# Gated MLP with quantised down projection: where down_w is rounded, how up_w rows are split, and how the split operands are laid out

## The chip, the cores and the metric

The kernel runs on one core of one Trainium2 chip. A time is that of one execution on the device, in microseconds (us). The engines are PE (matrix products), DVE (vector), ACT (scalar, activation functions), POOL (GpSimd) and SP, whose queue issues nearly all DMAs of this kernel. PEld is the loading of weights into PE.

## The reference, cut to what matters

For x of 4 x 1024 x 512, a condition of 4 x 128, up_w of 4096 x 512 and down_w of 512 x 2048, all float32:

```
scale = cond @ norm_w.T + 1.0
ms = jnp.mean(x * x, axis=-1, keepdims=True)
h = x * (scale[:, None, :] * jax.lax.rsqrt(ms + EPS))
u = h @ up_w.T
val, gate = jnp.split(u, 2, axis=-1)
h = val * jax.nn.gelu(gate, approximate=False)
hq = h + jax.lax.stop_gradient(act_quant(h) - h)
wq = down_w + jax.lax.stop_gradient(weight_quant(down_w) - down_w)
y = hq @ wq.T
return y + x
```

act_quant rounds each token's 2048 values to whole numbers from -128 to 127 with the token's own scale. weight_quant rounds down_w to -1, 0 or 1 with one scale, 1 over the mean of its absolute values.

## The kernel before, in words

The 4096 tokens are four batches of 1024, each two halves of 512 tokens. FF = 2048 is cut into 16 groups j of 128 rows (NJ), so one slot of the program makes one group: value and gate rows of up_w against the batch's tokens.

**Operands in two parts.** A float32 operand is split into a float16 "high" and a float16 "low" (the rest), and a product is high by low, low by high, and high by high. One matrix product of 512 columns takes about 0.216 us on PE.

**The first batch** (`first_batch(j)`, j = 0 to 15, from about 20 to 200 us) uses plain products: for each half `plain_half` runs 12 products for the gate (pg) and 12 for the value (pv), then ACT's Gelu (L604), then DVE's product L608, which writes H and so frees the PSUM bank "E" (two of them) that pv wrote. In the same slots the kernel prepares everything else, by an order written out by hand:

- *up_w, all groups.* `w_load` brings 128 gate and 128 value rows (L261), `w_range` finds each row's power of two (DVE, L269 to L284), `w_scale` applies it (POOL for j below ROWS = 8, ACT L295 from 8 on).
- *Groups 0 to 7* are transposed by PE (`w_turn`) and split when they leave PSUM (`w_high`, `w_low`).
- *Groups 8 to 15* are split as rows: `w_rows(j + 3)` at the end of slot j casts to float16 on ACT (L323), subtracts on DVE (L325), and one transposing DMA (L326) brings the result into the group's tile. It does so in three pieces, since the four quarters A11, A12 (gate) and A21, A22 (value) stand in the tile in another order than in the rows.
- *Sums.* For the later batches each group also needs four sums of its quarters (a product scheme with seven products in place of eight): `s_sums` (POOL, L359 to L362), `s_high` (ACT, L371), `s_low` (POOL, L375). `s_spill` writes the seven operands (C_ALL = 7 chunks of 2 x 256 float16 per partition) to DRAM (L379 to L384).
- *Tokens of the next batch* (class Tokens, four sets; load on SP L491, norm and scale in slots 6, 8, 10, 12, sums and split and turn in slots 7, 9, 11, 13). In the even slot: squares on ACT (L499), L473 on DVE, the power on POOL (L474), scaling on ACT (L507), DVE's L512. In the odd slot: sums on POOL (L520 to L523), casts on ACT (L544), subtractions on DVE (L548), a transposing DMA (L551). The buffer `xn` exists once, so the next set's load follows the subtractions.
- *down_w* comes in eight parts. `d_round(n)` (two DVE operations on 128x1024, L446 and L447) runs in slot 5 + n, `d_put(n)` (ACT, L456) one slot later; two parts make one tile, which `d_put` of an odd part sends through a transposing DMA (L458).

Within a slot the order on each engine is that of the code: on SP, for instance, the load of up_w, the spill, L458, L491, L551, then L326.

**Batches 1 to 3** run `slot(g)`, g = 16 to 63, with seven products of six matrix products each: 0, 4, 1, 5 and 6 in their own slot, 3 and 2 in the next. The operands come back from DRAM: `s_load_x` for 0, 1, 4, 5, 6 and `s_load_y` for 2 and 3, one and two slots ahead. The tile SXY has two places for groups; in the first batch a third lies in R (S_more). Group rows 8 to 15 were spilled untransposed where they are sums, and are turned by the load (L393). `SX` and `SY` say at which chunk an operand stands. Operand 2's low place is chunk 6; for groups 8 to 15 of the first batch that sum lies in the tile A21 instead.

**The down projection** of batch b - 1 runs in slots 10 to 13 of batch b (class Pair, also with seven products). It needs sums of the signs of down_w (T1 to T4, `d_sums`, DVE L469), made once in slots 9 and 10 of batch 1, and sums of the quantised tokens: `Pair.sum1` (DVE, L812) and `Pair.sums`. `more_sums` is what slot 9 runs between two products.

Of the kernel before, what the change touches and what calls it, by code (L numbers as in the profile page):

```python
# [9 lines left out]
F16 = mybir.dt.float16  # L10
# [4 lines left out]
ALU = mybir.AluOpType  # L15
# [19 lines left out]

C_ALL = 7

SX = {4: 0, 5: 1, 6: 2, 0: 3, 1: 4}
SY = {3: 0, 2: 1}

# [8 lines left out]
def glu_quant_kernel(  # L51
# [10 lines left out]
    PE, ACT, DVE, POOL, SP = nc.tensor, nc.scalar, nc.vector, nc.gpsimd, nc.sync  # L62
# [4 lines left out]
    HALF = D // 2  # L67
    NA = TOK // P
    NK = D // P
    NJ = FF // P  # L70
# [23 lines left out]
    H = cpool.tile([P, NSLOT, 2, TOK], F32, name="H")  # L94
# [3 lines left out]
    s_dram = tc.dram_tile([NJ, P, 7 * 2 * HALF], F16, name="s_dram")  # L98
# [7 lines left out]
    for n in range(0, P, 32):  # L106
        c = slice(n, n + 32)
# [6 lines left out]
    def t_view(b):  # L114
        v = R[:, b % 2].bitcast(F16)[:, : NA * C_ALL * 2 * HALF]
        return v.rearrange("p (a c l k t) -> p a c l k t", a=NA, c=C_ALL, l=2, k=2)
# [14 lines left out]
    A21 = R[:, 0, 6144 : 6144 + 768].bitcast(F16).rearrange("p (n w f) -> p n w f", n=3, w=2)  # L131

    def s_tile(g):


        if g >= NJ:
            return SXY[:, (g + 1) % 2]
        return S_more if g % 3 == 2 else SXY[:, g % 3]
# [111 lines left out]
    def wn(j):  # L250
        return H[:, W_SLOT[j % 3]]
# [28 lines left out]
    def w_range(j, t0=0, t1=2):  # L280
        w_factor(j, w_largest(j, t0, t1), t0, t1)
# [6 lines left out]
    ROWS = 8  # L288
# [20 lines left out]
    def a_parts(j):  # L309

        s = s_tile(j)
        return s[:, 3:5], s[:, 6] if j >= ROWS else A21[:, j % 3], s[:, 5]

    def w_row_parts(j):

        v = H[:, 15 + j % 2].bitcast(F16).rearrange("p t d -> p (t d)")
        v = v.rearrange("p (n w f) -> p n w f", n=4, w=2)
        f = wn(j).rearrange("p t (n f) -> p t n f", n=2)
        return (v[:, 0:2], f[:, 1]), (v[:, 2:3], f[:, 0, 1:2]), (v[:, 3:4], f[:, 0, 0:1])

    def w_rows(j):
        for o, f in w_row_parts(j):
            ACT.copy(o[:, :, 0], f)  # L323
        for o, f in w_row_parts(j):
            DVE.tensor_tensor(o[:, :, 1], f, o[:, :, 0], ALU.subtract)  # L325
        SP.dma_start_transpose(  # L326
            s_tile(j)[:, 3:7].rearrange("p n w (k f) -> p (n w k) f", k=2),
            H[:, 15 + j % 2].bitcast(F16).rearrange("p t d -> p (t d)"),
        )

    def w_high(j, ts=(1, 0)):
# [31 lines left out]

    def s_parts(j):
        s = s_tile(j)
        s4 = A21[:, j % 3 : j % 3 + 1] if j >= ROWS else s[:, 6:7]
        return (s[:, 0:3], sf[:, 0:3]), (s4, sf[:, 3:4])

    def s_high(j):
# [5 lines left out]
            eng.tensor_tensor(s[:, :, 1], f, s[:, :, 0], ALU.subtract)  # L375

    def s_spill(j):
        if j < ROWS:
            SP.dma_start(out=s_dram[j], in_=s_tile(j).rearrange("p c w f -> p (c w f)"))  # L379
            return  # L380
        SP.dma_start(
            out=s_dram[j, :, :Y_AT], in_=s_tile(j)[:, 0:6].rearrange("p c w f -> p (c w f)")
        )
        SP.dma_start(  # L384
            out=s_dram[j, :, Y_AT:], in_=A21[:, j % 3].rearrange("p w f -> p (w f)")
        )

    Y_AT = 6 * 2 * HALF

    def s_load(g, c0, c1, turn=False):  # L390
        s, d = s_tile(g)[:, c0:c1], s_dram[g % NJ, :, c0 * 2 * HALF : c1 * 2 * HALF]
        if turn:
            SP.dma_start_transpose(s.rearrange("p c w (k f) -> p (c w k) f", k=2), d)  # L393
        else:
            SP.dma_start(out=s.rearrange("p c w f -> p (c w f)"), in_=d)

    def s_load_x(g):
        if g % NJ < ROWS:
            s_load(g, 0, 5)
        else:  # L400
            s_load(g, 3, 5)
            s_load(g, 0, 3, True)

    def s_load_y(g):
        if g % NJ < ROWS:
            s_load(g, 5, 7)
        else:
            s_load(g, 5, 6)
            s_load(g, 6, 7, True)


    wmean = cpool.tile([P, 1], F32, name="wmean")
# [3 lines left out]
    ND = 2 * NK  # L416

    def d_part(n):
        return R[:, 1, n * HF : (n + 1) * HF]

    def d_at(n):

        return n // 4 + 2 * (n % 2), n // 2 % 2, n % 2
# [20 lines left out]
    def d_round(n):  # L444
        dn = d_part(n)
        DVE.tensor_scalar(dn, dn, wsc, 1.0, ALU.mult, ALU.min)  # L446
        DVE.tensor_scalar(dn, dn, -1.0, MAGIC, ALU.max, ALU.add)  # L447
# [3 lines left out]
    def d_put(n):  # L451
        _, u, y = d_at(n)
        if y == 0:
            tn.append(wpool.tile([P, HF], BF16, name=f"tn_{n}", tag="v"))
        t8 = tn[-1].bitcast(F8).rearrange("p (f y) -> p f y", y=2)
        ACT.activation(t8[:, :, y], d_part(n), AF.Copy, bias=-MAGIC, saturate=False)  # L456
        if y:
            SP.dma_start_transpose(wd[:, n // 4, u], tn[-1])  # L458

    def w_block(name):  # L460
        k, y = W_AT[name]
        return wd8[:, :, k, :, :, y]
# [3 lines left out]
    def d_sums(ns):  # L466
        for n, c in [(n, c) for n in ns for c in range(2)]:
            o, m, l = (w_block(name) for name in D_SUMS[n])
            DVE.tensor_tensor(o[:, c], m[:, c], l[:, c], ALU.subtract, saturate=False)  # L469
# [87 lines left out]
    TERMS = [(w, 1 - w, k) for w in (1, 0) for k in range(2)] + [(0, 0, k) for k in range(2)]  # L557

    def product(c, g, ps, start, stop):
        s = s_tile(g)[:, SX[c] if c in SX else 5 + SY[c]]  # L560
        s = s.rearrange("p w (k f) -> p w k f", k=2)
        tv = t_view(g // NJ)
        o = ps.rearrange("p (a t) -> p a t", t=P)
        for n, (w, l, k) in enumerate(TERMS):
            PE.matmul(  # L565
                o, s[:, w, k, :], tv[:, :, c, l, k, :],
                start=start and n == 0, stop=stop and n == len(TERMS) - 1,
                skip_group_check=True,
            )
# [428 lines left out]

    D_LOAD = {0: (4, 5), 1: (6, 7), 2: (0, 1), 3: (2, 3)}
    D_SUM = {1: (4, 5), 2: (6, 7), 3: (0, 1), 4: (2, 3)}  # L1000
    D_ROUND = {5 + n: n for n in range(ND)}
    TOKENS = {6: 0, 8: 1, 10: 2, 12: 3}
    PAIRS = {
        3: [(0, 0), (0, 1)], 4: [(1, 0), (1, 1)], 6: [(2, 0)], 7: [(2, 1)],
# [9 lines left out]
    def first_batch(j, sc):  # L1014

        if j + 4 < NJ:
            w_load(j + 4)
        for n in D_LOAD.get(j, ()):
            d_load(n)
        t = toks.get(j)  # L1020
        odd = t is not None and j not in TOKENS
        n = j + 2
        rows = ROWS <= n < NJ
        if j + 1 < ROWS:
            s_sums(j + 1)
        elif rows:
            s_sums(n)
        if odd:
            t.sums()
        if j + 3 < NJ:  # L1030
            w_range(j + 3)
            w_gain(j + 3)
        if j == 5:
            part = d_total()
        if j + 3 < ROWS:
            w_scale(j + 3)
        plain_half(j, 0)
        if j == 3:
            pd = cond_spread(dg, 1, B, "po")
            cond_undo(pd, 1, B)  # L1040
            cond_rows()
        pairs = PAIRS.get(j, ())
        for i, h in pairs[:2]:
            for f in pair_max(0, i, h):
                f()
        if j + 1 < ROWS:
            s_all(j + 1)
        elif rows:
            s_all(n)
        if n < ROWS:  # L1050
            w_turn(n)
            w_high(n)
            w_evac(n)
            w_low(n)
        if t and not odd:
            t.norm()
        if j - 1 in D_ROUND:
            d_put(D_ROUND[j - 1])
        if j in D_ROUND and j > 5:
            d_round(D_ROUND[j])  # L1060
        if t and not odd:
            t.scale(sc)
        if odd:
            t.high()
            t.low(DVE)
        if j + 1 in TOKENS:
            toks[j + 1] = toks[j + 2] = Tokens(1, TOKENS[j + 1])
            toks[j + 1].load()
        if odd:
            t.turn()  # L1070
        plain_half(j, 1)
        if j == 5:
            d_mean(part)
        if ROWS <= j + 3 < NJ:
            w_scale(j + 3)
            w_rows(j + 3)
        if rows and j + 1 < ROWS:
            s_sums(n)
            s_all(n)
        if j == 5:  # L1080
            d_round(D_ROUND[j])
        for i, h in pairs[2:]:
            for f in pair_max(0, i, h):
                f()
        for n in D_SUM.get(j, ()):
            d_sum(n)
        if j in (NJ - 3, NJ - 1):
            s_load_x(NJ + (j - NJ + 3) // 2)
            s_load_y(NJ + (j - NJ + 3) // 2)
# [177 lines left out]
    for b in range(1, B):  # L1267
# [45 lines left out]
        for j in range(NJ):  # L1313
            g = b * NJ + j
# [30 lines left out]
            def next_pair():  # L1345
                if b + 1 < B and j + 1 in DOWN:
                    pairs[j + 1] = Pair(b - 1, DOWN[j + 1])
                    pairs[j + 1].sum1(h_slots(g + 1)[:, 0, 0])

            def more_sums():  # L1350
                d_sums(late_sums)
                next_pair()

            mid = [nothing] * 3
            if j + 1 == min(DOWN):
# [148 lines left out]
    for h in range(2):  # L1504
# [19 lines left out]
        for a in range(NA):  # L1524
            c, xr = slice(0, HALF * ys[a]), XR[:, h * NA + a]
            down_mm(b, h, a, pos[a][:, c], range(cut, NJ), 0, ys[a])
            down_end(b, h, a, pos[a][:, c], xr[:, c], dq, c)
    c = slice(HALF, D)
# [29 lines left out]
```

## Time and profile before

| | us |
|---|---|
| three runs | 746.27, 743.80, 745.10 (median 745.1) |
| the profiled execution | 744.48 |
| its span, first to last instruction | 742.7 |
| PE's granted clock in all stretches | 1.00 |
| first batch on PE ends | 199.6 |
| DMAs from SP: operands of batches 1 to 3, first issue | 192.65 |

The span is what the profile's rows are measured in; the execution's own time has 1.8 us more. A line "101.20 1.36 DVE L325 ... x3" is a start, a length, an engine, a line of the program, the operation, output and input, and how many were merged; in brackets stands the engine's idle time before it and what ended it. In the waits, a line gives who waited for whom: total, times, longest. SPq is SP's queue. One answer serves to show the shapes of the rows' subtraction and how far its length varies (least, median, most, in ns):

```profile
L325 DVE TENSOR_TENSOR H<-H x24: 415/940/1859, 87.6 to 177.9; 128x256 f16<-128x256 f32 x16, 128x512 f16<-128x512 f32 x8
```

### The profile page before, as it was taken

What the parts mean: (1) busy time and instruction counts of PE and PEld (TensorE: products, weight loads), DVE (VectorE), ACT (ScalarE), POOL (GpSimd) and SP (SyncE); (2) the same over time, 40 slices, a digit from 0 to 9 for tenths busy, and PEclk for the clock granted to TensorE, in tenths of its full rate; (3) what the DMA queues carried; (4) which work ended last, traced back from release to release, by engine and by line L of the source; (5) the groups of instructions that cost most, each with busy time, mean ns of one, the idle gap of its engine ahead of it and who ended that gap; (6) DMA issues with size and microseconds to landing.
All of it is one profiled execution on the core that took longest, in us unless ns stands there. A gap on an engine that the chain in (4) does not pass through costs nothing.

```text
span 742.7 us, 10178 instructions
## 1 busy us (share of the span) xinstructions
PE 725.7 (98%) x3700; PEld 362.9 (49%) x3700; DVE 605.2 (81%) x865; ACT 392.4 (53%) x655; POOL 204.1 (27%) x205
## 2 busy tenths in 40 slices
PE   7999998889999999999999999999999999999998
PEld 3545443334444445566444445566444444445744
DVE  6968698987989888898679888687679888764897
ACT  5757646576235676453433667454433666333274
POOL 1499477886010030443010030444020000000100
PEclk9999999999999999999999999999999999999999
DMA  6289868987822456747933346657932335444253
GB/s 235 74 320 181 259 183 195 266 233 174 216 86 99 142 101 170 192 124 172 221 121 104 111 120 158 163 155 170 212 101 99 103 111 104 104 108 104 87 184 114
DMA packets 158414, 114.68 MB, mean 154 GB/s; under 512 B 124438, under 2 KB 129431, under 8 KB 158364
## 3 DMA queue, kind: packets, MB, share of 16 engines
q1 hardware_dynamic: 158074, 113.70, 57.7%
q8 instruction: 29, 0.48, 0.3%
q10 hardware_dynamic: 290, 0.33, 0.2%
q14 instruction: 21, 0.17, 0.1%
HBM read 62.08 MB, written 23.09 MB: 115 GB/s over the span
## 4 chain that ended last, share of the span: by engine, by line
PE 76%; DVE 3%; ACT 0%; issue 0%; DVEq 0%; ACTq 0%
PE A L565 33%; PE E L565 17%; PE B L565 8%; PE po L836 8%; PE po_end L785 4%; PE pv L580 2%; PE pg L580 2%; PE po L785 1%; DVE H L325 1%; DVE nx L548 0%; PE po_B L836 0%; DVE gm L699 0%; DVE wam L269 0%; DVE H L608 0%; PE po_A L836 0%
## 5 line engine op out<-in xcount | busy, mean ns | idle before, releaser
L565 PEld LDWEIGHTS <-SXY 128*128 128x128 f16 x2016 | 197.1, 98 | 232.8 <-DMA SXY<-s_dram 0.9
L565 PE MATMUL A<-R,SXY 128*128 128x512 f16 x1152 | 266.5, 379 | 0.1
L565 PE MATMUL E<-R,SXY 128*128 128x512 f16 x576 | 140.0, 379 | 0.1
L663 DVE SCALAR_TENSOR_TENSOR H<-A,sg,t 128x512 f32<-128x512 f32 x48 | 36.0, 750 | 71.7 <-PE A L565 71.5
L715 POOL PARTITION_ALL_REDUCE am<-R x8 | 14.3, 1793 | 226.6 <-DVE R L701 226.6
L757 DVE TENSOR_TENSOR H<-H,am 128x1024 f32<-128x1024 f32 x64 | 76.2, 1216 | 0.0
L580 PEld LDWEIGHTS <-SXY 128*128 128x128 f16 x438 | 42.8, 98 | 59.0 <-issue 8.9
L676 ACT ACTIVATE t<-t,sg 128x512 f32<-128x512 f32 x48 | 34.6, 721 | 69.5 <-DVE t L673 69.4
L565 PE MATMUL B<-R,SXY 128*128 128x512 f16 x288 | 70.0, 379 | 0.0
L699 DVE TENSOR_REDUCE gm<-H 128x512 f32<-128x1024 f32 x56 | 69.0, 1231 | 1.0
L474 POOL TENSOR_TENSOR rs<-ssq,neghalf 128x2 f32<-128x2 f32 (+1 forms) x13 | 12.5, 960 | 192.7 <-DVE ssq L473 192.7
L580 PE MATMUL pg<-R,SXY 128*128 128x512 f16 x252 | 57.8, 379 | 0.0
L836 PE MATMUL po<-wd,R 128*128 128x256 fp8e4 (+1 forms) x448 | 56.8, 275 | 0.0
L836 PEld LDWEIGHTS <-R 128*128 128x128 bf16 (+1 forms) x480 | 46.9, 98 | 12.8
L660 ACT ACTIVATE t<-B,sg 128x512 f32<-128x512 f32 x48 | 33.0, 687 | 36.5 <-PE B L565 36.5
L580 PE MATMUL pv<-R,SXY 128*128 128x512 f16 x186 | 45.3, 379 | 7.0 <-DVE H L608 7.0
L643 ACT COPY t<-A 128x512 f32<-128x512 f32 x48 | 27.9, 582 | 39.8 <-PE A L565 39.5
L651 ACT COPY B<-A 128x512 f32<-128x512 f32 x48 | 27.4, 572 | 39.3 <-PE A L565 38.8
L580 PEld LDWEIGHTS <-R 128*128 128x128 f16 x306 | 29.9, 98 | 36.6 <-issue 1.6
L765 ACT ACTIVATE H<-H 128x1024 f32<-128x1024 f32 x38 | 39.9, 1050 | 14.1 <-DVE H L757 11.1
L580 PE MATMUL pv<-R 128*128 128x512 f16 x186 | 45.4, 379 | 1.1 <-DVE H L608 1.1
L655 ACT COPY v<-E 128x512 f32<-128x512 f32 x48 | 28.1, 585 | 30.8 <-PE E L565 27.5
(192 smaller groups left out, 1025.4 us busy)
## 6 DMA issues: line engine op xcount, KB each, us to landing
SXY<-s_dram SPq DMA_DIRECT2D x24, 640.0 KB, 3.9
SXY<-s_dram SPq DMA_DIRECT2D x48, 256.0 KB, 4.2
H<-in_L_cond_up_w_dram SPq DMA_DIRECT2D x13, 512.0 KB, 6.6
s_dram<-SXY SPq DMA_DIRECT2D x6, 896.0 KB, 6.0
xr<-in_x_dram SPq DMA_DIRECT2D x19, 256.0 KB, 3.2
out_dram<-xr SPq DMA_DIRECT2D x19, 256.0 KB, 2.7
H<-in_x_dram SPq DMA_DIRECT2D x8, 512.0 KB, 5.3
R<-in_L_cond_down_w_dram SPq DMA_DIRECT2D x8, 512.0 KB, 7.0
```

Source lines behind the costliest of these rows:

```text
L565: PE.matmul(o, s[:, w, k, :], tv[:, :, c, l, k, :], start=start and n == 0, stop=stop and n == len(TERMS) - 1, skip_group_check=True,)
L580: PE.matmul(ps, a[k // 2][:, w, k % 2, :], XP[:, l, k, h * TOK : (h + 1) * TOK], start=n == 0, stop=n == len(terms) - 1,)
L643: ACT.copy(cur["t2"], cur["A"])
L655: ACT.copy(cur["v"], cur["E"])
L660: ACT.activation(cur["t1"], pb, AF.Gelu, scale=gain(g, 1))
L663: DVE.scalar_tensor_tensor(h_half(g - 1, 0), prev["A"], gain(g - 1, 0), prev["t1"], ALU.mult, ALU.mult)
L676: ACT.activation(prev["t2"], prev["t2"], AF.Gelu, scale=gain(g - 1, 1))
L699: DVE.tensor_reduce(gm[0], v, AX.X, ALU.max, apply_absolute_value=True)
L757: DVE.tensor_tensor(v, v, r.to_broadcast([P, 2, TOK]), ALU.mult)
L765: ACT.activation(v, v, AF.Copy, bias=MAGIC)
L785: PE.matmul(po.rearrange("p (y c o) -> p y c o", c=2, o=P), q[:, a, h, j], wd8[:, :, j // n, j % n, :, y0:y1].rearrange("p c o y -> p y c o"),
L836: PE.matmul(po, w[:, j], m, start=start and j == 0, stop=stop and j == n - 1, skip_group_check=True,)
```

## The change

Four edits. (1) The rounding of down_w: part 0 at the end of slot 5 as before, then parts 1 and 2 in slot 6, 3 and 4 in slot 8, 5 and 6 in slot 10, part 7 in slot 12; the puts follow one slot later. (2) `w_rows` casts and subtracts all four quarters with one operation each. (3) So that this is one step, the operands' chunks are ordered otherwise: 4, 5, 6, 2, 3, 0, 1 from chunk 0 on. What `s_load_x` brings (chunks 0 to 2 and 5 to 6) is now in two pieces for all groups, what `s_load_y` brings is chunks 3 and 4, and the spill of groups 8 to 15 has three pieces. (4) In slot 9 of batch 1 `next_pair` (with `sum1`) comes in front of the sums of signs.

```
-SX = {4: 0, 5: 1, 6: 2, 0: 3, 1: 4}
-SY = {3: 0, 2: 1}
+PLACE = {4: 0, 5: 1, 6: 2, 2: 3, 3: 4, 0: 5, 1: 6}
+Y_FROM, Y_TO = 3, 5
...
-        return s[:, 3:5], s[:, 6] if j >= ROWS else A21[:, j % 3], s[:, 5]
+        return s[:, 5:7], s[:, 3] if j >= ROWS else A21[:, j % 3], s[:, 4]
...
     def w_rows(j):
-        for o, f in w_row_parts(j):
-            ACT.copy(o[:, :, 0], f)
-        for o, f in w_row_parts(j):
-            DVE.tensor_tensor(o[:, :, 1], f, o[:, :, 0], ALU.subtract)
+        v = H[:, 15 + j % 2].bitcast(F16).rearrange("p t d -> p (t d)")
+        n = v.rearrange("p (n w f) -> p n w f", n=4, w=2)
+        f = wn(j).rearrange("p t (n f) -> p (t n) f", n=2)
+        ACT.copy(n[:, :, 0], f)
+        DVE.tensor_tensor(n[:, :, 1], f, n[:, :, 0], ALU.subtract)
         SP.dma_start_transpose(
-            s_tile(j)[:, 3:7].rearrange("p n w (k f) -> p (n w k) f", k=2),
-            H[:, 15 + j % 2].bitcast(F16).rearrange("p t d -> p (t d)"),
+            s_tile(j)[:, 3:7].rearrange("p n w (k f) -> p (n w k) f", k=2), v
         )
...
-        s4 = A21[:, j % 3 : j % 3 + 1] if j >= ROWS else s[:, 6:7]
+        s4 = A21[:, j % 3 : j % 3 + 1] if j >= ROWS else s[:, 3:4]
...
     def s_spill(j):
+        def out(c0, c1, v):
+            SP.dma_start(
+                out=s_dram[j, :, c0 * 2 * HALF : c1 * 2 * HALF],
+                in_=v.rearrange("p c w f -> p (c w f)"),
+            )
+
+        s = s_tile(j)
         if j < ROWS:
-            SP.dma_start(out=s_dram[j], in_=s_tile(j).rearrange("p c w f -> p (c w f)"))
+            out(0, C_ALL, s)
             return
-        SP.dma_start(
-            out=s_dram[j, :, :Y_AT], in_=s_tile(j)[:, 0:6].rearrange("p c w f -> p (c w f)")
-        )
-        SP.dma_start(
-            out=s_dram[j, :, Y_AT:], in_=A21[:, j % 3].rearrange("p w f -> p (w f)")
-        )
+        out(0, 3, s[:, 0:3])
+        out(4, C_ALL, s[:, 4:])
+        out(3, 4, A21[:, j % 3 : j % 3 + 1])
...
     def s_load_x(g):
-        if g % NJ < ROWS:
-            s_load(g, 0, 5)
-        else:
-            s_load(g, 3, 5)
-            s_load(g, 0, 3, True)
+        s_load(g, Y_TO, C_ALL)
+        s_load(g, 0, Y_FROM, g % NJ >= ROWS)
 
     def s_load_y(g):
         if g % NJ < ROWS:
-            s_load(g, 5, 7)
+            s_load(g, Y_FROM, Y_TO)
         else:
-            s_load(g, 5, 6)
-            s_load(g, 6, 7, True)
+            s_load(g, Y_FROM + 1, Y_TO)
+            s_load(g, Y_FROM, Y_FROM + 1, True)
...
-        s = s_tile(g)[:, SX[c] if c in SX else 5 + SY[c]]
+        s = s_tile(g)[:, PLACE[c]]
...
-    D_ROUND = {5 + n: n for n in range(ND)}
+    D_ROUND = {5: (0,), 6: (1, 2), 8: (3, 4), 10: (5, 6), 12: (7,)}
...
-        if j - 1 in D_ROUND:
-            d_put(D_ROUND[j - 1])
-        if j in D_ROUND and j > 5:
-            d_round(D_ROUND[j])
+        for m in D_ROUND.get(j - 1, ()):
+            d_put(m)
+        for m in D_ROUND.get(j, ()) if j > 5 else ():
+            d_round(m)
...
         if j == 5:
-            d_round(D_ROUND[j])
+            d_round(0)
...
             def more_sums():
+                next_pair()
                 d_sums(late_sums)
-                next_pair()
```

More of the change, by code (lines that the diff above doesn't have):

```diff
@@ L311, in a_parts, with w_rows @@
         s = s_tile(j)
-        return s[:, 3:5], s[:, 6] if j >= ROWS else A21[:, j % 3], s[:, 5]
-    def w_row_parts(j):
+        return s[:, 5:7], s[:, 3] if j >= ROWS else A21[:, j % 3], s[:, 4]
+    def w_rows(j):
         v = H[:, 15 + j % 2].bitcast(F16).rearrange("p t d -> p (t d)")
[L317 to L321, printed above, removed]
-        for o, f in w_row_parts(j):
-            ACT.copy(o[:, :, 0], f)
-        for o, f in w_row_parts(j):
-            DVE.tensor_tensor(o[:, :, 1], f, o[:, :, 0], ALU.subtract)
+        n = v.rearrange("p (n w f) -> p n w f", n=4, w=2)
+        f = wn(j).rearrange("p t (n f) -> p (t n) f", n=2)
+        ACT.copy(n[:, :, 0], f)
+        DVE.tensor_tensor(n[:, :, 1], f, n[:, :, 0], ALU.subtract)
         SP.dma_start_transpose(
-            s_tile(j)[:, 3:7].rearrange("p n w (k f) -> p (n w k) f", k=2),
-            H[:, 15 + j % 2].bitcast(F16).rearrange("p t d -> p (t d)"),
+            s_tile(j)[:, 3:7].rearrange("p n w (k f) -> p (n w k) f", k=2), v
         )
@@ L377, in s_spill @@
     def s_spill(j):
+        def out(c0, c1, v):
[4 more added lines that the diff above has]
+        s = s_tile(j)
         if j < ROWS:
-            SP.dma_start(out=s_dram[j], in_=s_tile(j).rearrange("p c w f -> p (c w f)"))
+            out(0, C_ALL, s)
             return
-        SP.dma_start(
-            out=s_dram[j, :, :Y_AT], in_=s_tile(j)[:, 0:6].rearrange("p c w f -> p (c w f)")
-        )
-        SP.dma_start(
-            out=s_dram[j, :, Y_AT:], in_=A21[:, j % 3].rearrange("p w f -> p (w f)")
-        )
-    Y_AT = 6 * 2 * HALF
+        out(0, 3, s[:, 0:3])
+        out(4, C_ALL, s[:, 4:])
+        out(3, 4, A21[:, j % 3 : j % 3 + 1])
     def s_load(g, c0, c1, turn=False):
```

## The prediction

> **What bounds the kernel now.** I read the busy times first, then who waits for whom, then the chain of waits, then each engine in order of time between 90 and 200 us.
>
> ```profile
> PE 725.7 (98%) x3700; PEld 362.9 (49%) x3700; DVE 605.2 (81%) x865; ACT 392.4 (53%) x655; POOL 204.1 (27%) x205
> ```
>
> TensorE is the bound nearly everywhere, so only time in which it stands still can be won. The waits between 100 and 175 us hold most of that:
>
> ```profile
> PE pv L580 <- DVE H L608: 8.0, 9, 1.7
> ```
>
> A value product (pv) waits nine times for the DVE product L608 that empties the bank of two half slots earlier. A half slot (a gate and a value product) starts every 5.18 us where nothing stalls (86.50 to 107.22 us holds four). From 107.22, sixteen halves would end at 107.22 + 16 x 5.18 = 190.1; they end at 199.56. So 9.46 us are lost (the view says 8.0, since the modelled end of a product overlaps the next start by 0.16 each time). From 200 us to the end the same view has only 0.6 us of PE waiting. **9.46 us is all that this stretch can give.**
>
> ```profile
> 112.00:172.00 60.00, 51.98 (x236) 22.84 (x235) 54.10 (x73) 39.94 (x73) 46.59 (x44) 1.00 0.93 235
> 172.00:200.00 28.00, 28.00 (x132) 12.64 (x131) 23.02 (x27) 12.12 (x20) 11.42 (x12) 1.00 0.77 193
> ```
>
> Columns: stretch, length, busy PE, PEld, DVE, ACT, POOL, clock, DMA share, GB/s. Here DVE is busy for 54.1 of 60 us, POOL for 46.6, and the DMA engines for 0.93: three resources near their end at once. The chain of waits runs through DVE at just this place:
>
> ```profile
> 152.33 2.60 DVE H L325 x3
> 160.90 3.70 DVE nx L548 x3
> 165.26 3.24 DVE H L325 x3
> 171.07 2.75 PE pv L580 x12
> ```
>
> DVE in order of time (slot 9 begins at 118.36 on PE, but DVE runs one and a half halves behind; its slot 9 is about 131 to 144.5, slot 10 to 154.9):
>
> ```profile
> 101.20 1.36 DVE L325 TENSOR_TENSOR H<-H 128x512 f16<-128x512 f32 x3
> ...
> 128.45 2.60 DVE L325 TENSOR_TENSOR H<-H 128x512 f16<-128x512 f32 x3 [0.42 <-ACT H L323]
> ...
> 134.30 0.75 DVE L446 TENSOR_SCALAR R<-R,wsc 128x1024 f32<-128x1024 f32 x1
> 135.08 2.02 DVE L447 TENSOR_SCALAR R<-R 128x1024 f32<-128x1024 f32 x1
> ...
> 141.30 3.33 DVE L325 TENSOR_TENSOR H<-H 128x512 f16<-128x512 f32 x3
> ...
> 147.12 0.74 DVE L446 TENSOR_SCALAR R<-R,wsc 128x1024 f32<-128x1024 f32 x1
> 147.90 0.69 DVE L447 TENSOR_SCALAR R<-R 128x1024 f32<-128x1024 f32 x1
> 150.03 1.22 DVE L512 TENSOR_TENSOR xn<-xn,sc 128x1024 f32<-128x1024 f32 x1 [1.44 <-ACT xn L507]
> ```
>
> L447 takes 0.69 us in slot 10 and 2.02 in slot 9; the three L325 take 1.36 in all at 101 us and 3.33 at 141. The difference is POOL:
>
> ```profile
> 134.45 3.17 POOL L375 TENSOR_TENSOR R<-H,R 128x768 f16<-128x768 f32 x2
> ...
> 142.52 1.82 POOL L375 TENSOR_TENSOR SXY<-H,SXY 128x768 f16<-128x768 f32 x1
> ...
> 151.93 0.72 POOL L359 TENSOR_TENSOR H<-H 128x256 f32<-128x256 f32 x1 [3.30 <-issue]
> ```
>
> While POOL runs one of its instructions, these DVE operations wait for its end, and the other way round: they alternate, one whole instruction each. In slots 8, 10 and 12 POOL pauses (3.30 us before 151.93) just while DVE rounds, and DVE then idles 1.44 us.
>
> **The change part by part.**
>
> *Rounding.* The parts rounded in slots 7, 9 and 11 cost 2.32 (108.12 to 110.44), 2.76 and 2.76 us of DVE there. Moved to slots 6, 8 and 10 they cost 0.74 + 0.69 + 0.04 of gaps = 1.47 each where POOL is quiet; in slots 8 and 10 this falls into the idle 1.44, net 0.03. In slot 6 POOL already runs its sums (four L359 to L362 from 97.20), so there I take the contended 2.3, less 1.44 idle: +0.9. If the idle cover were gone, the price would be 1.47 a slot. DVE net: -7.84 + 0.06 + 0.9 = -6.9. The put (L456, 1.04 on ACT) of the moved part goes from the even slot, where it hides behind the wait for POOL's L474, to the odd slot ahead of L544. In slot 9 the copies of xn end at 133.8 and the one of xt starts at 134.5 after a wait of 0.7 for POOL; 1.04 more makes it 0.3 late (bounds 0 and 1.04). The transposes that SP issues for it (L458) stay in slots 7, 9, 11, 13.
>
> *Rows in one step.* Sixteen ACT casts and sixteen DVE subtractions go. ACT: 1.22 becomes 1.05 (L544 on 128x1024), -0.17 a slot. DVE: one operation of 1024 waits for POOL at most once instead of three times. Uncontended it is 1.22 (L548, L512), with one wait 1.75 (L548 on xt). I take 1.75: odd slots 2.91, 3.33, 3.32 give 4.3 us together. Even slots 8 and 10: it must wait for the whole cast (1.05, not 0.61 for the first third), so 0.42 + 2.60 becomes 0.86 + 1.22 to 1.75: 0.4 to 0.9 each, say 1.2 together. DVE -5.5.
>
> *Places.* Loads of the first eight rows' X part become two (24 more on SP), each spill of rows 8 to 15 three instead of two (8 more); bytes stay. An issue takes SP 0.33 to 0.57. In the loops of batches 1 to 3 a load lands in about 4 us and is wanted a 9 us slot later: nothing. The first, at 192.65, landed at 196.86 for a PE start of 199.56; now the part wanted first is issued first and is smaller: nothing, with 2.7 us of cover. The new spill is issued while SP waits for POOL's last L375: nothing, bound 0.35 a slot.
>
> [...] Here they come from SP, a 640 KB load lands in 3.9 us (median) and a 256 KB one in 4.2, and they overlap.
>
> *Slot 9's sum.* L812 ran at 287.25 to 287.94, PE wanted it at 289.01 and did not wait. 2.3 us sooner gives nothing; the signs' sums, 0.68 later, are first used a slot later. It may meet ACT's L769 that ends at 285.62: at most 0.6 on DVE, none on PE. Zero.
>
> **The sum.** DVE would be relieved of 6.9 + 5.5 = 12.4 us, more than the 9.46 lost. But another loop comes up: the next tokens have one buffer.
>
> ```profile
> 117.45 0.52 SPq L491 DMA_DIRECT2D xn<-in_x_dram  x1
> ...
> 137.66 0.33 SPq L384 DMA_DIRECT2D s_dram<-R  x1
> 138.04 1.81 SPq L458 DMA_TRANSPOSE wd<-tn  x1
> 139.94 0.59 SPq L491 DMA_DIRECT2D xn<-in_x_dram  x1
> ```
>
> From the issue at 117.45 it takes 4.3 to land, then squares, power, scaling, w_scale on ACT until POOL's L359 at 128.05: 10.60. POOL needs 9.58 until the end of its last L375 (137.63). SP then issues L384 and L458 before the next load: 2.31. Together 22.5 us, and PE needs only 20.72 for two slots. The second turn, to 163.68, took 23.74, of which 1.4 was DVE coming late to L473. The change takes little from the loop itself: the contention of L447 with L375 (0.5) goes, that of L548 takes its place. So 22.4 a turn.
>
> The first issue comes sooner: in slot 7 POOL's L520 to L522 took 1.18 each instead of 0.72 because of the rounding (-1.4) and L375 on R waited 1 us; against that slot 6 hands on about 0.6. I take 1.1 (bounds 0.6 and 1.85): 116.35, then 138.75, 161.15. L359 of slot 13 follows 10.6 later, 171.75, and the second L608 of slot 13 ends 10.33 after it (175.81 to 186.14 now): 182.1. PE without stalls wants it at 109.81 + 13 x 5.18 = 177.15. **About 5.0 us of stall stay**; L608 of slots 10 and 12, where two small DVE operations each wait for an L375, may add 0.3. Gain 9.46 - 5.2 = 4.2 us. The profiled execution took 744.48 (span 742.7 and 1.8 around it): 740.3. It lies 0.6 under the median of 745.1, by which it would be 740.9. I say **740.5**; own range, by the bounds of the first issue and of the waits, 739 to 742.
>
> **The rivals.** *DVE's work alone decides.* If POOL, less disturbed, shortens the loop to 20.7, all 9.46 come back: 735.0 to 737. For it: 12.4 is more than 9.46. Against it: 9.58 of the loop is POOL's own work, and POOL has gaps of 3.3 only because it waits for this chain. 0.18.
>
> *A full neighbour.* The stretch gets shorter with the same bytes; at a DMA share of 0.93, 4 us of 60 less make 1.0. Loads and transposes (L551 holds SP for 5.2 us) then land later; each turn loses about 0.7, or all chances between L275, L284 and L375 fall badly: gain 0.5 to 2.2, 743.5. 0.17.
>
> *Slower: the put in front of the tokens' cast.* In slots 7, 9 and 11 ACT does two puts before L544. If POOL's sums are ready first, L548, the next load and L608 are each late by 1.04: 3 x 1.04 = 3.1, 747.6. It decides where L544 on xt ends after both L375. Against it: ACT had 0.7 of waiting in slot 9 and 2.36 in slot 7. 0.08.
>
> *It does not do what it says:* the pairs meet POOL in all even slots, +0.9 each, and the odd slots' gain of 2.8 is halved: about 742.5. 0.05.
>
> The forecast has 0.52. **The numbers:** 0.3% is 2.2 us, about what can be told from no change. Faster by more: 0.50 of the forecast's 0.52, 0.18, 0.05 of the full neighbour and 0.03 of the last, 0.76. Within: 0.02 + 0.12 + 0.02 = 0.16. Slower: 0.08. The range from 736.8 to 743.6 leaves out most of the slower case, the best of the first rival and the edge of the second.
>
> **What would show it.** Right: no L447 over 1.2 us in slots 9 and 11; L325 once a slot at 1.2 to 1.8 us; L446 and L447 twice over before L512 in slots 8, 10, 12 with its idle 1.44 gone; PE's wait for L608 near 4 us, in slots 10 to 13 rather than from 8 on; L491 every 22.4 us. Wrong: L491 closer than 21.5 (then more is won), L608 waiting behind L548 behind L544 without POOL in between (then the put costs), a wait of PE for a load at the start of batch 1.

## The result, and the profile after

| | us |
|---|---|
| before, 11 runs beside the changed kernel | 745.05 (743.8 to 746.27) |
| changed kernel, 11 runs | 741.93 (740.29 to 744.67) |
| ratio, 95% interval | 0.9961 [0.9948, 0.9974] |
| profiled execution of the changed kernel | 742.59, span 740.8 |
| the changed kernel once more, beside other experiments | 741.74 against 746.01, 0.9938 [0.9915, 0.9961] |

By the medians the change gains 3.1 us in the one comparison and 4.3 in the other. In the new kernel the line numbers fall by 5 to 7: L580 is now L573, L608 is L601, L565 is L558, L375 is L369, L359 is L353, L548 is L541, L325 is L320, L446 and L447 are L439 and L440, L512 is L505, L491 is L484, L458 is L451, L551 is L544. The kernels below that issue a load first have one line more, so L574, L602, L452, L485 and L545 there.

The busy times and PE's largest wait, read as before:

```profile
PE 726.9 (98%) x3700; PEld 364.2 (49%) x3700; DVE 599.5 (81%) x849; ACT 391.4 (53%) x639; POOL 203.0 (27%) x205
```

```profile
PE pv L573 <- DVE H L601: 4.4, 7, 1.3
```

The wait of a value product for DVE goes from 8.0 to 4.4 us. Two rows of PE in order of time place it between two marks, the product for the mean of down_w (at 86.36 in the profile of before) and the first product of batch 1 (at 199.56):

```profile
88.13 0.28 PE L433 MATMUL pmean<-wpart,one 128*128 128x1 f32 x2
...
197.94 1.46 PE L558 MATMUL A<-R,SXY 128*128 128x512 f16 x6
```

From mark to mark it took 113.20 us and now takes 109.81: 3.39 less. With 9.46 us of stall before, this stretch would take 113.20 - 9.46 = 103.74 without any, so 6.07 us of stall are left now. All stalls below are measured in this way, from mark to mark. From the second mark to the end of the span it was 543.13 and is 542.85: 0.28 less. The stretch up to the first mark is 1.77 longer, and that is not the change: PE's clock was lower at the start of this execution, as the first of these two stretches shows (columns as in the prediction):

```profile
0.00:20.00 20.00, 14.56 (x60) 7.42 (x61) 12.03 (x59) 10.54 (x22) 3.16 (x8) 0.91 0.64 213
112.00:172.00 60.00, 55.62 (x253) 24.61 (x252) 51.86 (x64) 40.29 (x67) 47.12 (x45) 1.00 0.95 240
```

It was 1.00 in the first 20 us of before, and is 1.00 in the other profile of the changed kernel, whose first mark stands at 86.70. So 1.77 - 3.39 - 0.28 = -1.90, and the profiled executions differ by 742.59 - 744.48 = -1.89. The sum closes: the change itself is worth 3.39 + 0.28 = 3.67 us here. In the other profile of the changed kernel, by the same marks, it is worth 3.3 (a stall of 6.43). In the second stretch PE is busy for 3.6 of 60 us more than before, DVE for 2.2 less.

The loop of tokens on SP's queue, with the transposing DMA that goes ahead of the load:

```profile
116.63 1.75 SPq L451 DMA_TRANSPOSE wd<-tn  x1
118.88 0.40 SPq L484 DMA_DIRECT2D xn<-in_x_dram  x1
...
141.28 0.53 SPq L484 DMA_DIRECT2D xn<-in_x_dram  x1
...
164.03 0.54 SPq L484 DMA_DIRECT2D xn<-in_x_dram  x1
```

The loads follow one another after 22.40 and 22.75 us (22.49 and 23.74 before); the time from one of them to the next is called a turn below. Now DVE in slot 8 and one line of slot 9, with one line of POOL in front:

```profile
121.01 1.64 POOL L369 TENSOR_TENSOR SXY<-H,SXY 128x768 f16<-128x768 f32 x1
121.22 1.45 DVE L284 TENSOR_SCALAR sg<-sw,dx 128x2 f32<-128x2 f32 x1
...
126.19 0.75 DVE L439 TENSOR_SCALAR R<-R,wsc 128x1024 f32<-128x1024 f32 x1
126.97 0.69 DVE L440 TENSOR_SCALAR R<-R 128x1024 f32<-128x1024 f32 x1
127.72 1.23 DVE L505 TENSOR_TENSOR xn<-xn,sc 128x1024 f32<-128x1024 f32 x1
...
141.05 1.77 DVE L320 TENSOR_TENSOR H<-H 128x1024 f16<-128x1024 f32 x1
```

The second pair of roundings costs 0.75 and 0.69, and L505 follows at once, without the 1.44 us of idle time. The rows' subtraction stands once, at 1.77. But L284, which handles two elements per partition, takes 1.45 us: it ends with POOL's L369. Before, the same line met nothing:

```profile
121.62 0.21 DVE L284 TENSOR_SCALAR sg<-sw,dx 128x2 f32<-128x2 f32 x1
```

The groups of DVE between the two marks show this in sum (busy time, mean ns of one, then idle time before it and what ended it; L541 has a second group, on xt, with 5.9 us):

```profile
L320 DVE TENSOR_TENSOR H<-H 128x1024 f16<-128x1024 f32 x8 | 12.3, 1537 | 3.0 <-ACT H L319 3.0
L541 DVE TENSOR_TENSOR nx<-xn,nx 128x512 f16<-128x512 f32 (+1 forms) x8 | 10.2, 1315 | 6.0 <-ACT nx L537 6.0
...
L284 DVE TENSOR_SCALAR sg<-sw,dx 128x2 f32<-128x2 f32 x7 | 6.3, 897 | 0.0
```

Counted from single rows between the marks, the rows' subtraction went from 21.32 to 12.29 us and L440 from 8.61 to 5.96. L284 went from 2.54 to 6.28 and L541 from 14.99 to 16.38. All of DVE went from 106.81 to 99.78. **Of 11.7 us that two edits took off DVE's instructions, 5.1 came back on two others**, because the waits for POOL moved to whichever DVE instruction comes next. And DVE now idles 6.0 us before L541 on xn, where it idled 1.9.

### The profile page after: what moved, and what is told of

Its sections match the earlier page's. It is cut to its first block, busy times and chain, and to the rows that moved or that the text cites. A ratio compares the mean times of both kernels' runs of the same rounds, so it can differ in the third digit from the quotient of the medians.

```text
span 740.8 us, 10208 instructions
## 1 busy us (share of the span) xinstructions
PE 726.9 (98%) x3700; PEld 364.2 (49%) x3700; DVE 599.5 (81%) x849; ACT 391.4 (53%) x639; POOL 203.0 (27%) x205
## 4 chain that ended last, share of the span: by engine, by line
PE 72%; DVE 2%; POOL 1%; issue 1%; ACT 0%; DVEq 0%; POOLq 0%
PE A L558 32%; PE E L558 16%; PE po L829 8%; PE B L558 8%; PE po_end L778 4%; PE pv L573 1%; PE po L778 1%; PE pg L573 1%; DVE gm L692 1%; PE po_B L829 0%; DVE R L694 0%; DVE R L687 0%; PE po_A L829 0%; POOL H L355 0%; DVE H L805 0%
## 5 line engine op out<-in xcount | busy, mean ns | idle before, releaser
L558 PEld LDWEIGHTS <-SXY 128*128 128x128 f16 x2016 | 197.2, 98 | 232.3 <-issue 0.6
L558 PE MATMUL A<-R,SXY 128*128 128x512 f16 x1152 | 266.3, 379 | 0.0
L558 PE MATMUL E<-R,SXY 128*128 128x512 f16 x576 | 140.0, 379 | 0.1
L558 PE MATMUL B<-R,SXY 128*128 128x512 f16 x288 | 70.0, 379 | 0.0
L573 PEld LDWEIGHTS <-SXY 128*128 128x128 f16 x438 | 42.8, 98 | 55.4 <-issue 5.4
L573 PE MATMUL pg<-R,SXY 128*128 128x512 f16 x252 | 57.8, 379 | 0.0
L573 PE MATMUL pv<-R,SXY 128*128 128x512 f16 x186 | 45.3, 379 | 3.5 <-DVE H L601 3.5
L573 PEld LDWEIGHTS <-R 128*128 128x128 f16 x306 | 29.9, 98 | 36.8 <-issue 2.0
L573 PE MATMUL pv<-R 128*128 128x512 f16 x186 | 45.4, 379 | 1.0 <-DVE H L601 0.9
```

Source lines behind the costliest of these rows:

```text
L558: PE.matmul(o, s[:, w, k, :], tv[:, :, c, l, k, :], start=start and n == 0, stop=stop and n == len(TERMS) - 1, skip_group_check=True,)
L573: PE.matmul(ps, a[k // 2][:, w, k % 2, :], XP[:, l, k, h * TOK : (h + 1) * TOK], start=n == 0, stop=n == len(terms) - 1,)
```

## The experiments

Ratios are to runs of the kernel before on the same chip: 746.49 for the first four, 746.01 for the second four, 745.81 for the next three, 745.59 for the last.

**Rounding alone** (edit 1 on the kernel before).

```
-    D_ROUND = {5 + n: n for n in range(ND)}
+    D_ROUND = {5: (0,), 6: (1, 2), 8: (3, 4), 10: (5, 6), 12: (7,)}
...
```

> Theory (token loop: load of the next tokens to the next such load, 22.4 us a turn, caps the gain): the rounding alone takes DVE's lateness of 1.4 us out of the second turn, and DVE still does three row subtractions a slot; 1.5 to 3 us faster than before (ratio 0.996 to 0.998), L447 never over 1.3 us in slots 9 and 11, loads of tokens 22.4 us apart. Rival (DVE's work decides): DVE is relieved of 6.9 us, so 5 to 7 us faster. Rival (rows alone bring the gain): no change.

Measured: 742.24, 0.9940 [0.9919, 0.9962], by the medians as much as the whole change and more than the 1.5 to 3 us of the theory, though less than the rival's 5 to 7. The turns are 23.02 and 22.72, not 22.4. Its profiled execution (743.83) is slower than its median, with DVE's L269 of slot 6 starting 2.0 us later than in the profile of before, so its stall of 8.55 is not compared.

This lateness is not the edit. At the end of slot 5 POOL's L375 (L369 in the new kernel) starts 4.4 to 4.5 us after the first mark in every profile, and DVE comes there with its last operations at about the same time. In nine of the fourteen profiles DVE's L240 goes first and L269 of slot 6 starts 4.1 to 4.7 us after the mark. In this profile POOL goes first, L240 takes 1.91 us in place of 0.48, and L269 starts at 6.27. Places alone and the first profile of load first, both with one pair in slot 5 as well, have it in the same way.

**Rows in one step alone** (edits 2 and 3).

```
-    D_ROUND = {5: (0,), 6: (1, 2), 8: (3, 4), 10: (5, 6), 12: (7,)}
+    D_ROUND = {5 + n: (n,) for n in range(ND)}
...
-                next_pair()
                 d_sums(late_sums)
+                next_pair()
```

(against the changed kernel)

> The rows in one step and the new places, with the rounding as before and slot 9 as before. Theory (token loop): DVE is relieved of 5.5 us, but POOL in slots 7, 9, 11 still meets the rounding; 1 to 2.5 us faster than before (0.9966 to 0.9987). Rival (DVE's work decides): 5 us faster. Rival (the rounding alone brings the gain): no change.

Measured: 744.46, 0.9977 [0.9962, 0.9991]. That is within the theory's 1 to 2.5 us, but the trace does not show its reason. DVE's busy time between the marks falls from 106.81 to 100.36, nearly as far as in the changed kernel, but the stall is 9.48 us, as before. Its largest wait and its loop:

```profile
PE pv L573 <- DVE H L601: 8.0, 7, 1.7
```

```profile
140.89 0.56 SPq L484 DMA_DIRECT2D xn<-in_x_dram  x1
164.70 0.61 SPq L484 DMA_DIRECT2D xn<-in_x_dram  x1
```

From 118.01 on the turns take 22.88 and 23.81, together 0.5 us more than before. Here 6.45 us less work on DVE was worth nothing on PE, while the loop of tokens did not get shorter.

**Places alone** (the chunks' order, loads and spills of edit 3, with the rows cast and subtracted in three steps, and the rounding and slot 9 as before; the cut is against the changed kernel).

```
-        ACT.copy(n[:, :, 0], f)
-        DVE.tensor_tensor(n[:, :, 1], f, n[:, :, 0], ALU.subtract)
+        cuts = (slice(2, 4), slice(1, 2), slice(0, 1))
+        for c in cuts:
+            ACT.copy(n[:, c, 0], f[:, c])
+        for c in cuts:
+            DVE.tensor_tensor(n[:, c, 1], f[:, c], n[:, c, 0], ALU.subtract)
...
```

> The new places alone: rows still in three steps, rounding and slot 9 as before, so 32 more DMAs and nothing else. Theory: within 0.5 us of before (0.9993 to 1.0007). Rival (a full neighbour: the added DMA of each spill delays what SP issues behind it in slots 7, 9, 11): 0.5 to 2 us slower than before.

Measured: 744.86, 0.9980 [0.9965, 0.9995]: the 32 more DMAs cost nothing by the medians. The theory had no change within 0.5 us, and the 1.6 us gained lie outside that. The profiled execution is the slowest of twelve (748.40), with L269 of slot 6 at 6.26 and a stall of 11.43, so its stall is not compared. The 0.28 us after the second mark appears in each profile with the new places and in none with the old ones. The other 1.35 us of the medians have no place in the trace, and stay open. Against this kernel the rows in one step bring 0.0003 of the time, which is nothing.

**Load first** (the changed kernel, with SP's transposing DMA of a down_w tile issued behind the load of the next tokens).

```
-            SP.dma_start_transpose(wd[:, n // 4, u], tn[-1])
+            turns.append(lambda t=tn[-1]: SP.dma_start_transpose(wd[:, n // 4, u], t))
...
+        while turns:
+            turns.pop(0)()
```

> The changed kernel, with the transposing DMA of down_w (L451) issued behind the load of the next tokens (L484) in slots 7, 9 and 11, not ahead of it. Theory (token loop): each load is issued 1.2 to 1.8 us sooner, the loop falls from 22.4 to about 21, and the stalls of PE on L601 from 4.4 us to 1 to 2: about 3 us faster than the changed kernel, 739 us (ratio to before 0.991 to 0.993). Rival (DVE's work decides what is left): as the changed kernel, 742 (0.996). Rival (DMA engines are full): the loads land later by what they are issued sooner, 742.

Measured: 739.57, 0.9907 [0.9883, 0.9930], and a second time 740.16, 0.9916 [0.9897, 0.9936]. The two profiles differ. The first, of the slowest execution of its six (742.91), has POOL ahead of DVE at the end of slot 5, two rows of which are shown here:

```profile
90.37 2.72 POOL L369 TENSOR_TENSOR SXY<-H,SXY 128x768 f16<-128x768 f32 x2 [4.72 <-ACT SXY L365]
90.41 2.15 DVE L440 TENSOR_SCALAR R<-R 128x1024 f32<-128x1024 f32 x1
```

There L269 of slot 6 starts 7.40 us after the first mark, the first load comes at 30.80, the turns are 21.62 and 23.71, and the stall is 8.63. In the second profile these are 4.13, 28.50, 21.47 and 21.94, and the stall is 4.62. What the edit moves is the same in both: the first load comes 0.57 and 0.58 us after the end of POOL's last L369 of slot 7, in place of 2.83 in the changed kernel. A new wait stands in the second profile:

```profile
133.49 1.22 DVE L269 TENSOR_REDUCE wam<-H 128x2 f32<-128x1024 f32 x1 [1.82 <-DMA H<-in_L_cond_up_w_dram]
...
154.80 1.22 DVE L269 TENSOR_REDUCE wam<-H 128x2 f32<-128x1024 f32 x1 [1.09 <-DMA H<-in_L_cond_up_w_dram]
```

**The changed kernel again**, and **slot 9's sum back** (edit 4 undone).

```
-                next_pair()
                 d_sums(late_sums)
+                next_pair()
```

> The changed kernel itself, to be compared on one chip with the next three and with the rounding alone. Theory: ratio to before 0.995 to 0.997 as measured, so the rounding alone (0.994) is at least as good as all four edits. Rival (the edits add up): 0.992 to 0.994, better than the rounding alone.

> The changed kernel with the signs' sums in front of the sum of slot 9 again, as before the change. Theory: within 0.5 us of the changed kernel, since PE did not wait for that sum. Rival: 0.6 to 2 us slower, if PE's bank or DVE behind it depended on the order.

Measured: 741.74, 0.9938 [0.9915, 0.9961], with a stall of 6.43 us; and 741.35, 0.9935 [0.9911, 0.9960], with 6.29. Edit 4 is worth nothing. The 0.9938 lies in the rival's range, not in the theory's, but it is not better than the 0.9940 of the rounding alone. With intervals of some 1.7 us to either side, the two do not settle whether the other edits add anything to the rounding.

**Puts late** (the changed kernel, with ACT's two puts of an odd slot behind the tokens' casts).

```
-        for m in D_ROUND.get(j - 1, ()):
-            d_put(m)
+        if not odd:
+            for m in D_ROUND.get(j - 1, ()):
+                d_put(m)
...
+            for m in D_ROUND.get(j - 1, ()):
+                d_put(m)
```

> The changed kernel with the puts of slots 7, 9, 11 and 13 on ACT behind the cast of the tokens (L537) instead of in front of it. Theory (token loop): the first two subtractions L541 then fall among POOL's sums and delay POOL's L369 by as much as they win; within 0.7 us of the changed kernel, or up to 1.5 us slower. Rival (the put in front of the cast costs about 1 us in each of three slots): 1 to 3 us faster.

Measured: 743.68, 0.9966 [0.9950, 0.9983], 1.9 us more than the changed kernel, a little beyond the theory's 1.5. ACT at slot 9:

```profile
135.07 1.05 ACT L537 CAST nx<-xt 128x1024 f16<-128x1024 f32 x1 [1.63 <-POOL xt L516]
136.02 2.00 ACT L449 ACTIVATE tn<-R 128x1024 fp8e4<-128x1024 f32 x2
```

The casts now wait 1.63 us for POOL, which the puts used to fill; and the puts end at 138.02, so that L451 starts at 138.62 and the load behind it at 140.44. As the theory has it, the earlier subtractions also hold POOL up: its last L369 of slot 7 ends 28.88 us after the first mark, not 27.92. The turns are 22.95 and 23.10, the stall 8.32. In this kernel putting first is better than putting last; puts last together with the load first was not run.

**Part 1 early** (the changed kernel with parts 0 and 1 in slot 5, so that slot 6 has one pair).

```
-    D_ROUND = {5: (0,), 6: (1, 2), 8: (3, 4), 10: (5, 6), 12: (7,)}
+    D_ROUND = {5: (0, 1), 6: (2,), 8: (3, 4), 10: (5, 6), 12: (7,)}
...
```

> The changed kernel with parts 0 and 1 rounded at the end of slot 5 and part 2 alone in slot 6, so that no slot rounds beside POOL's sums. Theory (the pair in slot 6 meets POOL's sums, and that ate the gain of the first load): L439 and L440 at 0.75 and 0.69 in slot 6, the first load (L484) 0.8 to 1.8 us sooner after slot 6's first L269 than in the changed kernel (26.6 us there), and the kernel 0.5 to 1.8 us faster than the changed one. Rival (slot 6 is without weight): no change.

Measured: 742.25, 0.9944 [0.9926, 0.9963]; the expected gain did not come. The stall is 7.09, and DVE's L269 of slot 6 starts 7.35 us after the first mark, not 4.13: the second pair in slot 5 meets POOL (L440 2.09). The pair was no cheaper there, only earlier in the way: it brings about by the program's order what chance brought about in the first profile of load first.

**Both loads first** (load first, and in odd slots the load of up_w for group j + 5 ahead of the tokens' transposing DMA).

```
+        if odd and j + 5 < NJ:
+            w_loaded.add(j + 5)
+            w_load(j + 5)
...
```

> The changed kernel with two issues moved on SP: the load of the next tokens goes ahead of the transposing DMA of down_w's tile (as in the kernel with the load first), and in odd slots up_w's load for group j + 5 is issued ahead of the tokens' transposing DMA, not behind it in the next slot. Theory (the order of issues on SP holds both loops): DVE's waits at L269 for up_w, 2.16 and 1.33 us in the kernel with the load first alone, are gone (under 0.4 each), the next tokens' loads follow one another in 20.7 to 21.5 us, PE's stall before batch 1 falls by 1 to 2 us against that kernel, and the time is 737.5 to 738.8. Rival (the DMA engines are full there, with a share of 0.95 to 1.02): up_w lands just as late although it is issued sooner, since it shares the engines with the turn, and the time stays at 739.3 to 740.2.

> The kernel with the tokens' load first once more, as the comparison on the same chip: 739.0 to 740.2 by both theories, and waits of DVE at L269 for up_w of more than 1 us in two of the slots 8 to 12.

Measured: 738.42, 0.9897 [0.9877, 0.9917], the fastest of all kernels here. SP at the end of slot 7:

```profile
114.76 0.95 SPq L485 DMA_DIRECT2D xn<-in_x_dram  x1
115.76 0.51 SPq L261 DMA_DIRECT2D H<-in_L_cond_up_w_dram  x1
116.70 1.25 SPq L452 DMA_TRANSPOSE wd<-tn  x1
118.06 5.66 SPq L545 DMA_TRANSPOSE R<-nx  x1
```

L545 holds SP for 5.66 us; the two loads ahead of it went out at 114.76 and 115.76, and the first issue behind it starts at 123.84. In this profile no L269 from slot 7 on waits for up_w, and the stall is 3.70 us, 0.92 less than in the second profile with the tokens' load alone ahead (1 to 2 were expected), while the DMA engines' share from 112 to 172 us is 0.99 against 1.00. So it was the order of the issues, and not full DMA engines. Turns of 21.39 and 22.84 are not the 20.7 to 21.5 of the theory.

**All three** (both loads first, and parts 0 and 1 in slot 5).

> The kernel before this one, with part 1 of down_w rounded in slot 5, so that slot 6 has only one pair. Theory (slot 6's contention sets the first turn of the loop once the loads are no longer in the way): 0.3 to 0.9 us faster than without it. Rival (POOL's sums, not DVE, set when the first tokens' load may be issued, as in the changed kernel, where the same edit gave nothing): within 0.4 us of it.

Measured: 741.13, 0.9936 [0.9916, 0.9955]: 2.7 us slower than without it, which neither theory had. Rows of DVE, of PE and of a stretch of 2 us:

```profile
91.29 2.02 DVE L440 TENSOR_SCALAR R<-R 128x1024 f32<-128x1024 f32 x1
```

```profile
117.76 4.19 PE L574 MATMUL pv<-R 128*128 128x512 f16 x12 [2.78 <-DVE H L602]
```

```profile
118.00:120.00 2.00, 2.00 (x6) 0.76 (x5) 1.82 (x2) 0.74 (x2) 2.00 (x3) 0.50 1.02 288
```

As in the kernel with part 1 early, the second pair in slot 5 meets POOL (2.02), L269 of slot 6 starts 7.84 us after the first mark, and PE waits 2.78 us in slot 8 already; the stall is 6.23. Then the granted clock falls to 0.50, and twelve products take 4.19 us where 2.75 is usual. How much of the longer stall these 1.4 us make is not separated, since PE waits for DVE again at 140.31.

**Parts later** (both loads first; part 1 alone in slot 6, then two parts in slots 8, 10 and 12).

```
-    D_ROUND = {5: (0,), 6: (1, 2), 8: (3, 4), 10: (5, 6), 12: (7,)}
+    D_ROUND = {5: (0,), 6: (1,), 8: (2, 3), 10: (4, 5), 12: (6, 7)}
```

> The kernel with both loads ahead, and the rounding moved the other way: part 1 alone in slot 6, parts 2 and 3 in slot 8, 4 and 5 in slot 10, 6 and 7 in slot 12. Slot 6 then has one pair on DVE, not two (its second pair took 1.22 and 1.10 us against POOL in the changed kernel), slot 5 keeps its one, and slot 12 has two where DVE idles anyway. Theory (slot 6's second pair holds up the first of the tokens' turns): POOL's last L369 of slot 7 and the load after it come 0.5 to 1.2 us sooner after the mean's product, and the ratio to before falls by 0.0007 to 0.0016 from the 0.9897 of that kernel, to 737.2 to 738.0. Rival (POOL's own sums of slots 6 and 7 set that load, and DVE's pair hides behind them): load within 0.3 us, ratio within 0.0005 of it, 738.1 to 738.8. In neither does DVE's L269 of slot 6 start later than 4.2 us after the mean's product, as it did with two pairs in slot 5.

Measured: 740.78, 0.9927 [0.9907, 0.9947]; neither theory holds. DVE has 2.3 us less to do in slot 6, and the first load comes 0.57 us *later* after the first mark (29.06 against 28.49). POOL's last operation of slot 7 in this kernel:

```profile
116.18 1.65 POOL L369 TENSOR_TENSOR R<-H,R 128x256 f16<-128x256 f32 x1
```

The same operation takes 0.85 us with both loads first. There DVE's L542 on xn and on xt follow without a gap; here L542 on xt begins at 115.54, right after an idle 0.83 us, and L369 has to wait for it. But this is not what the longer stall comes from, for the next turns make it good: the third load comes 72.33 us after the first mark, against 72.72 with both loads first. The stall is 4.25 us against 3.70, and the difference stands in slot 13, where PE does not wait with both loads first:

```profile
184.21 2.75 PE L574 MATMUL pv<-R 128*128 128x512 f16 x12 [0.59 <-DVE H L602]
```

Two parts rounded in slot 12 mean two puts ahead of L538 in slot 13 (2.00 us on ACT, not 1.05). DVE idles 3.61 us before L542 on xn there, not 2.67, and from POOL's L353 to the end of L602 it takes 11.50 us, not 10.62. So 0.55 of the 2.4 us of the medians is in the trace. The rest stays open, beyond the fact that this profiled execution had a clock of 0.83 in its first 20 us; the two kernels were not run on one chip, and their intervals overlap.

## Why the prediction was right, and where its working was off

**The bound and the kind of gain were right.** PE's stalls before batch 1 were what could be won. The forecast, 4.2 us gained with some 5 of stall left, stands against 3.1 and 4.3 measured and 3.67 in the trace. The 740.5 stands against 741.93, which is just inside the range of 739 to 742: about 1 us more stall stayed than the sum had.

**The loop of tokens, not DVE's work, is what caps it: shown from both sides.** With rows in one step alone DVE loses 6.45 us of busy time and PE gains none of it back; with the loads moved on SP, DVE's busy time stays (99.48 against 99.78) and the stall falls from 6.07 to 3.70. The turn of 22.4 us was met (22.40, then 22.75). This refutes the rival that DVE's work alone decides.

**The first issue: the term of the sum that was mis-sized.** The prediction moved it 1.1 us sooner (bounds 0.6 and 1.85). Measured from the first mark it came at 30.75 instead of 31.09, 0.34 sooner, outside these bounds. The two other profiles with the same order of issues agree (30.98 for the changed kernel again, 30.75 with edit 4 undone). The 0.76 us that are short of the 1.1 are most of the 1.07 us by which 6.07 exceeds the 5.0 predicted; the second turn, 22.75 for 22.4, gives the other 0.35; from the third load on the working holds (10.28 and 10.63 for 10.6 and 10.33). Why it came late is visible on SP. POOL's last L369 of slot 7 did end 1.3 us sooner after the mark (27.92 for 29.23), but the transposing DMA L451 then took 1.75 us where the row of before had 1.27, and 0.5 us lie between it and L484, for which the trace names no cause. From the end of L369 to the load it takes 2.83 us in place of 1.86, and 0.40 to 0.58 in all five profiles with the load ahead of L451, whether the load then comes at 28.49 (both loads first) or at 31.79 (all three). So L451 ahead of the load was the obstacle.

**Rounding: right, and by the medians the whole gain.** No L440 takes over 1.1 us between the marks, the pairs of slots 8 and 10 stand clean in front of L505 (idle time 0.05), and slot 6's second pair met POOL at 1.22 and 1.10 as assumed. Alone it gave 4.2 us by the medians (746.49 to 742.24), and the whole change 3.1 and 4.3. That it is the whole gain is not shown beyond the width of these intervals, since the trace of the rounding alone was late in slot 6. One sign of the prediction does not fit its own edit: slot 12 has part 7 alone, and the idle 1.44 us before L505 stays there; the third slot with two pairs is slot 6.

**Rows in one step: the relief of DVE was right, what it is worth was not.** I put the relief at 12.4 us. DVE's busy time fell by 7.0, and the idle time before L512 (now L505), which was to be filled, from 5.7 to 1.5: together 11.2. But of this the runs show no gain in time for the rows: their own 9.0 us less came back as 5.1 on L284 and L541, and as 4.1 more of idle time before L541 on xn, where DVE waits for ACT.

**Places and slot 9's sum: nothing, as costed.** 32 more DMAs did not cost by the medians (744.86 for the places alone, 746.49 for before); batch 1 started with no wait for a load. Edit 4 undone gave 741.35 for 741.74.

**The put in front of the cast** is no loss in slots 7, 9 and 11: placed behind, the kernel is 1.9 us slower. Its cover is the wait for POOL's sums, 1.63 us in slot 9 where the put does not fill it. In slot 13 that cover is short: with a second put there the way from L353 to L602 is 0.9 us longer (parts later), nearly the 1.04 of the rival. The *full neighbour* did not come either: the turns did not grow by 0.7, and the fastest kernel has a DMA share of 0.99 against 0.95.

**Where the stalls stand.** I expected them in slots 10 to 13. They begin in slot 8, with 1.1 us at 29.7 after the first mark. There L601 stands behind three L541 of slot 7, which alternate with POOL from 24.6 to 29.0; the prediction had not followed that half slot.

## What to carry to other kernels

Where a loop with one buffer crosses several engines, time the loop itself, from issue to issue of its load, and ask of each edit whether it shortens that; an engine's busy time can fall by 6 us beside it and win nothing. Look at what stands ahead of such a load in its issuing queue: moving two loads past transposing DMAs won some 3 us (0.9938 to 0.9897 of before), about as much again as the change itself. And where two engines hold each other up by whole instructions, an instruction taken away can pass its wait to the next one (5.1 of 11.7 us here), so a local saving has to be followed to the end of the slot before it is counted. Before two profiles are compared, check which of the two engines went first at such a place: the same kernel, load first, had its first load at 28.50 in the profile where DVE did and at 30.80 in the one where POOL did.

## What the runs showed of the hardware

**Whole instructions alternated, and one of two elements waited as well.** L284 with two elements per partition goes from 0.21 to 1.45 us beside a POOL L369 of 1.64. Not every operation of DVE got longer beside POOL: the reductions L269 take 1.20 to 1.22 us everywhere, also the one at 119.41 in the profile of the changed kernel (1.21), beside POOL's L355 and L356, and L601 takes 0.73 to 0.75, also the one at 117.05 (0.74), beside L353; L320 takes 1.21 to 1.77. Why the one kind waited and the other did not, the traces do not show. How much the order of arrival did at one place, they do: when POOL's L369 went first at the end of slot 5, DVE's L440 took 2.15 us in place of 0.69, and L269 of slot 6 started 7.40 us after the first mark, not 4.13.

**After two of three waits of some 3 us PE's clock was halved.** Beside the 2.78 us in the kernel with all three, two rows of PE from the first profile of load first:

```profile
117.92 2.75 PE L574 MATMUL pv<-R 128*128 128x512 f16 x12 [3.18 <-DVE H L602]
...
137.29 4.16 PE L574 MATMUL pv<-R,SXY 128*128 128x512 f16 x12 [3.31 <-DVE H L602]
```

After 3.31 us twelve products take 4.16 (the granted clock is 0.50 from 138 to 140 us), after 3.18 the usual 2.75, and after 2.78 they took 4.19 (0.50 from 118 to 120 us). So the length of the wait alone did not decide, and what did is not shown; where the clock fell, the products behind the pause took 1.4 us more.

**The clock at the start varied between executions.** In the first 20 us it was 0.83 or 0.91 in four profiles (the changed kernel, places alone, load first the second time, parts later) and 1.00 in before and others, and the first mark then came at 88.1 to 89.2 instead of 85.9 to 86.7. Read by the spans alone, the profiles of before and of the changed kernel would have hidden half of the change's 3.67 us.
